# A two-layer lookup convolution: from image-by-image stages with running maxima to layer-by-layer blocks with packed 32-column products

## The chip, the cores and the metric

The kernel runs on one core of a Trainium2 chip. A core has five engines that work side by side, each with its own queue in order: TensorE (PE, matrix products into PSUM; its weight loads are listed as PEld), VectorE (DVE), ScalarE (ACT), GpSimd (POOL) and SyncE (SP, which here issues transfers). [...] The metric is the device time of one execution in microseconds (us); the median of three runs before the change is 5095.48 us (5089.49 to 5102.17).

## The reference

The input x has 16 images of 256 channels, 28 x 28 pixels. It is normalized in 32 groups of channels, and a block with two approximated 3x3 convolutions follows. Each convolution has, for every channel, 16 code vectors of 9 numbers, compares each 3x3 patch of that channel with them, and takes a soft choice:

```python
def amm_conv3x3(x, centroids, w_sub, stride=1):
    B = x.shape[0]
    C, k, s = centroids.shape                      # 256, 16, 9
    patches = conv_general_dilated_patches(x, (3, 3), (stride, stride), 'SAME')
    p = patches.reshape(B, C, s, Ho * Wo).transpose(0, 3, 1, 2)
    d = sum(p * p, -1)[..., None] - 2.0 * einsum('bncs,cks->bnck', p, centroids) + sum(centroids ** 2, -1)
    attn = softmax(-d, axis=-1)
    lut = einsum('cks,cso->cko', centroids, w_sub)
    out = einsum('bnck,cko->bno', attn, lut)
    return out.transpose(0, 2, 1).reshape(B, -1, Ho, Wo)

out = relu(bn(amm_conv3x3(gn(x), centroids1, wsub1)))
out = bn(amm_conv3x3(out, centroids2, wsub2))
out = se_layer(out)                                # channel gates from the channel means
y = x + relu(out + gn(x))
```

In both kernels the lookup is taken apart: the exponentials of a channel's 16 logits are multiplied by its code vectors (the numerators, 9 rows for a channel), these are divided by the sum of the exponentials, and the quotient is multiplied by `w_sub`. The logit of code c for patch p is 2(p.c - |c|^2/2); the term |p|^2 falls out of the softmax. All data are fp32, in which a matmul is two instructions.

## The kernel before

Channels are laid three to a strip of 32 rows (27 rows of numerators, three of sums), four strips to a stack of 128: 88 strips, 22 stacks, taken two at a time (`g`, 11 of them). An image and layer is a stage, cut into 384 and 400 pixels; layer 1 of the next image and layer 2 of this one alternate. A pair of stacks and a cut of pixels is a slot, 704 in all; a unit is two slots.

Patches come from DRAM. `shift` on POOL makes the two sideways shifts of an image, `to_home` writes three shifted images, `to_pat` (L278) copies these within DRAM into a tensor of patches with a row of ones, and `patches` (L342) loads a unit.

For a safe exponential, each channel's maximum is subtracted. This makes logits twice: `a_logits` (L355) makes them, `a_turn` (L371) turns them in blocks of 32x32 on DVE, `a_max` (L379) takes the maxima over 16 codes, and `m_turn`, `m_out` (L397) and `m_in` (L406) carry the maxima by way of DRAM (dm) into rows of the patch tile, where the second product `b_logits` (L355 again) subtracts them. `b_exp` (L420) makes the exponentials on ACT, `b_num` (L429) the numerators and, in every eighth row, the sums; `b_keep` (L442) copies them to SBUF as q. The sums go by DRAM (ds, dr; L447 to L468) into a dense tile, where `r_make` (L457, L458) inverts them, and come back; `c_scale` spreads them over the rows with a shuffle on DVE (L481) and multiplies on POOL (L482). `c_look` (L491) multiplies by `w_sub` over all stacks into two banks, and `evacuate` (L507, L517) applies the batch norm. `se_hidden`, `se_gate`, `finish` and `store` end an image.

The order on each engine is written out by hand: `at(slot, half, f)` lists every step under a slot and a position in it, and the steps are issued in sorted order. A step of slot s stands at s (first logits), s + 3 (second), s + 4 (numerators), s + 8 and s + 9 (scaling, lookup). Six PSUM banks form one ring, `bank`; two more are the lookup's accumulators.

Of the kernel before, what the change touches and what calls it, by code (L numbers as in the profile page):

```python
# [8 lines left out]
F32 = mybir.dt.float32  # L9
AF = mybir.ActivationFunctionType  # L10
# [8 lines left out]
NPAD = (H + 2) * W  # L19
K = 16  # L20
NCH = 3
NRT = 88
NT = NRT // 4
NG = NT // 2
CPAD = NRT * NCH
GN_EPS = 1e-5
BN_EPS = 1e-5

PROW = [(v, 8) for v in range(7)] + [(24, 1), (27, 1)]
ONE = 30
MROW = (7, 15, 23)

NROW = [r for r in range(32) if r % 8 != 7][:27]

PXT = ((0, 384, 0, 384), (384, 400, 368, 416))
UNITS = ((0, 2), (2, 2), (4, 2), (6, 2), (8, 2), (10, 1))  # L40


def prow(j, s):
    base, step = PROW[j * 3 + s % 3]
    return base + step * (s // 3)
# [3 lines left out]
def kernel(  # L49
# [4 lines left out]
    cw1: bass.AP,  # L54
    ws1: bass.AP,
    wd2: bass.AP,
    cw2: bass.AP,
    ws2: bass.AP,
    nhalf: bass.AP,
    mones: bass.AP,  # L60
# [6 lines left out]

# [7 lines left out]
    drot = ctx.enter_context(tc.tile_pool(name="drot", bufs=3, space=DRAM))  # L82
    small = ctx.enter_context(tc.tile_pool(name="small", bufs=3))
    p_acc = ctx.enter_context(tc.tile_pool(name="p_acc", bufs=1, space=PSUM))
    p_ring = ctx.enter_context(tc.tile_pool(name="p_ring", bufs=6, space=PSUM))
# [8 lines left out]
    def view(t, off, dims):  # L94

        return bass.AP(t.tensor, t.offset + off, [list(d) for d in dims])


    DX = CPAD * NPAD
    d_home = [dram.tile([3 * CPAD, NPAD], F32, name=f"home{i}") for i in range(2)]  # L100
    d_pat = [dram.tile([NRT * 32, HW], F32, name=f"pat{i}") for i in range(3)]
    d_zero = dram.tile([2, NPAD], F32, name="zero")
# [3 lines left out]
    xpool = ctx.enter_context(tc.tile_pool(name="xpool", bufs=2))  # L106

    def load_x(b):
        t = xpool.tile([P, NB, HW], F32, tag="xt", name="xt")
        nc.gpsimd.dma_start(t, x[b].rearrange("(b p) n -> p b n", p=P))  # L110
        xs[b] = t

    xs = {}
    load_x(0)

    def zeros(dims):
        return view(d_zero, 0, dims)

    def clear_home(i):
        t = d_home[i]
        nc.scalar.dma_start(view(t, 0, [[NPAD, 3 * CPAD], [29 * W, 2], [1, W]]), zeros([[0, 3 * CPAD], [0, 2], [1, W]]))
        nc.scalar.dma_start(view(t, C * NPAD, [[DX, 3], [NPAD, CPAD - C], [1, NPAD]]), zeros([[0, 3], [0, CPAD - C], [1, NPAD]]))

    def clear_pat(i):
        t = d_pat[i]
        nc.scalar.dma_start(view(t, 7 * HW, [[32 * HW, NRT], [8 * HW, 4], [1, HW]]), zeros([[0, NRT], [0, 4], [1, HW]]))
        nc.scalar.dma_start(view(t, ONE * HW, [[32 * HW, NRT], [1, HW]]), view(d_zero, NPAD, [[0, NRT], [1, HW]]))

    with tc.tile_pool(name="zo", bufs=1) as zpool:
        zo = zpool.tile([2, NPAD], F32, name="zo")
        nc.vector.memset(zo, 1.0)
        nc.vector.memset(zo[0:1], 0.0)
        nc.scalar.dma_start(d_zero, zo)
    clear_home(0)
    clear_pat(0)


    nc.vector.tensor_scalar_mul(gmat, gmat, 1.0 / 8.0)  # L140
    mhalf = const.tile([P, NB], F32, name="mhalf")
    nc.vector.memset(mhalf, -0.5)

    def load(ap, name):
        t = const.tile(list(ap.shape), F32, name=name)
        nc.sync.dma_start(t, ap)
        return t

    vecs = load(vec, "vecs")
    nhalf_sb = load(nhalf, "nhalf_sb")  # L150
    mones_sb = load(mones, "mones_sb")
    wd = [load(wd1, "wd0")]
    cw = [load(cw1, "cw0")]
    ws = [load(ws1, "ws0")]
    wd.append(load(wd2, "wd1"))
    cw.append(load(cw2, "cw1"))
    ws.append(load(ws2, "ws1"))
# [5 lines left out]
    nb2_sb = const.tile([P, NB], F32, name="nb2_sb")  # L163
    nc.vector.tensor_scalar_mul(nb2_sb, vecs[:, :, 8], -1.0)

    def rsqrt(dst, src, eps, n):

        t = small.tile([P, n], F32, name="rs_t")
        nc.gpsimd.tensor_scalar(t, src, eps, None, op0=ALU.add)
        nc.gpsimd.tensor_tensor(dst, t, mhalf[:, :n], ALU.pow)  # L170


    bn = []
    for l in range(2):
        ga, be, mu, va = (vecs[:, :, 4 * l + i] for i in range(4))
        sc = const.tile([P, NB], F32, name=f"bnsc{l}")
        sh = const.tile([P, NB], F32, name=f"bnsh{l}")
        rsqrt(sc, va, BN_EPS, NB)
        nc.vector.tensor_mul(sc, sc, ga)
        nc.vector.tensor_mul(sh, mu, sc)  # L180
        nc.vector.tensor_sub(sh, be, sh)
        bn.append((sc, sh))


    def setup_codes(l):
        wf = wd[l].rearrange("p t m -> p (t m)")
        n = NT * 64
        for c0 in range(0, n, 416):
            m = min(416, n - c0)
            sq = tpool.tile([P, 416], F32, tag="z", name="sq")  # L190
            nc.gpsimd.tensor_tensor(sq[:, :m], wf[:, c0 : c0 + m], wf[:, c0 : c0 + m], ALU.mult)  # L191
            ps = bank("sqp")
            nc.tensor.matmul(ps[:, :m], lhsT=nhalf_sb, rhs=sq[:, :m], start=True, stop=True)  # L193
            nc.vector.tensor_add(wf[:, c0 : c0 + m], wf[:, c0 : c0 + m], ps[:, :m])
        nc.vector.tensor_add(wd[l], wd[l], mones_sb.unsqueeze(1).to_broadcast([P, NT, 64]))

    hpool = ctx.enter_context(tc.tile_pool(name="hpool", bufs=1))
    ppool = ctx.enter_context(tc.tile_pool(name="ppool", bufs=5))
    tpool = ctx.enter_context(tc.tile_pool(name="tpool", bufs=4))
    epool = ctx.enter_context(tc.tile_pool(name="epool", bufs=6))  # L200
    npool = ctx.enter_context(tc.tile_pool(name="npool", bufs=4))
    rpool = ctx.enter_context(tc.tile_pool(name="rpool", bufs=2))
    mxs = [const.tile([P, 8, 32], F32, name=f"mx{i}") for i in range(2)]
    for t in mxs:
        nc.vector.memset(t, 0.0)

    sides = {dx: const.tile([P, NB, HW], F32, name=f"side{dx}") for dx in (0, 2)}
    for t in sides.values():
        nc.gpsimd.memset(t, 0.0)


    gst = {}
    nrm = {}

    def gn_stats(b):
        st = small.tile([P, NB, 2, 6], F32, name="gn_st")
        mv = small.tile([P, NB, 2], F32, name="gn_mv")
        for k in range(NB):
            for i in range(2):
                nc.vector.bn_stats(st[:, k, i, :], xs[b][:, k, i * (HW // 2) : (i + 1) * (HW // 2)])  # L220
            nc.vector.bn_aggr(mv[:, k, :], st[:, k])
        gst[b] = mv

    def gn_mean(b):
        mv = gst[b]
        ps = bank("gnp")[:, : 2 * NB]
        nc.tensor.matmul(ps, lhsT=gmat, rhs=mv.rearrange("p b t -> p (b t)"), start=True, stop=True)
        gm = small.tile([P, NB, 2], F32, name="gn_gm", bufs=6)
# [6 lines left out]
    def gn_var(b):  # L235
        gm, dv = gst.pop(b)
        ps = bank("gnp")[:, :NB]
        nc.tensor.matmul(ps, lhsT=gmat, rhs=dv, start=True, stop=True)
        var = small.tile([P, NB], F32, name="gn_var")
        nc.vector.tensor_add(var, gm[:, :, 1], ps)  # L240
        rstd = small.tile([P, NB], F32, name="gn_rstd", bufs=6)
        rsqrt(rstd, var, GN_EPS, NB)
        nrm[b] = gm, rstd

    homes = {}

    def gn_apply(b):
        gm, rstd = nrm[b]
        xt = xs.pop(b)
        for k in range(NB):  # L250
            nc.gpsimd.tensor_scalar(  # L251
                xt[:, k], xt[:, k], gm[:, k, 0:1], rstd[:, k : k + 1], op0=ALU.subtract, op1=ALU.mult
            )
        homes[0, b] = xt


    def pat_of(l, b):
        if l == 0:
            return d_pat[2 if b == 1 else 0]
        return d_pat[0 if b == B - 1 else 1]  # L260

    def shift(l, b, dx, k):

        img = homes[l, b][:, k].rearrange("p (r w) -> p r w", w=W)
        to = sides[dx][:, k].rearrange("p (r w) -> p r w", w=W)
        if dx == 0:
            nc.gpsimd.tensor_copy(to[:, :, 1:W], img[:, :, 0 : W - 1])
        else:
            nc.gpsimd.tensor_copy(to[:, :, 0 : W - 1], img[:, :, 1:W])

    def to_home(l, b, dx):
        src = homes[l, b] if dx == 1 else sides[dx]
        nc.gpsimd.dma_start(view(d_home[l], dx * DX + W, [[NPAD, P], [P * NPAD, NB], [1, HW]]), src)

    def to_pat(l, b, n):
        dx, j = (1, 0, 2)[n // 3], n % 3
        base, step = PROW[j * 3 + dx]
        nc.gpsimd.dma_start(  # L278
            view(pat_of(l, b), base * HW, [[32 * HW, NRT], [step * HW, 3], [1, HW]]),
            view(d_home[l], dx * DX + j * NPAD, [[3 * NPAD, NRT], [W, 3], [1, HW]]),  # L280
        )


    ys = {}
    se = {}
# [391 lines left out]
```

## Time and profile before

| what | value |
|---|---|
| median time | 5095.48 us |
| span of the profiled execution | 5090.5 us |
| busy: PE / DVE / POOL / ACT | 86 / 74 / 44 / 42 % |
| mean granted TensorE clock | 0.919 |
| instructions: all / PE | 107493 / 39696 |
| DMA packets, bytes | 698762, 885.87 MB |
| lookups L491, busy and mean of one | 2408.2 us, 552 ns |
| logits L355, busy and mean of one | 1536.6 us, 553 ns |
| products L482 on POOL, busy and mean of one | 1400.7 us, 1012 ns |
| transposes L371 on DVE | 1435.6 us, 567 ns |
| maxima L379 on DVE | 1396.0 us, 560 ns |
| exponentials L420 on ACT | 1185.8 us, 515 ns |
| first logits start at | 114.2 us |

Busy time is the union of the intervals in which an engine has some instruction under way. Matmuls overlap, so the mean length of one is longer than the distance between the starts of two in succession, and packed matmuls of different strips run at the same time. What ends an idle stretch is shown per group and in the list of waits; the chain shows through which work the last instruction was reached.

### The profile page before, as it was taken

The numbers are of one execution on the slowest core, as the hardware profiler recorded it, in microseconds if no ns is written. First come the engines' busy times: TensorE is split into PE (matmuls) and PEld (weight loads), VectorE is DVE, ScalarE is ACT, GpSimd is POOL, SyncE is SP. The second block draws the span as 40 slices with busy tenths as digits, with TensorE's granted clock in tenths as the row PEclk, the third lists the DMA queues.
The fourth block names the chain that finished last, engine by engine and source line by source line (L and its number), as shares of the span: only waits on it lengthen the run. The fifth ranks groups of instructions, "written<-read, shape, count | busy, mean of one in ns | idle before, by whom it ended". The sixth has DMA issues, their size and how long they took to land. (4 is left out here: it accounts for less than half of the span.)

```text
span 5090.5 us, 107493 instructions
## 1 busy us (share of the span) xinstructions
PE 4396.4 (86%) x39696; PEld 1579.5 (31%) x39696; DVE 3769.4 (74%) x9144; ACT 2113.9 (42%) x5265; POOL 2254.7 (44%) x2438
## 2 busy tenths in 40 slices
PE   1788898888988889898898988889888898888988
PEld 0233333333333333233333333333233333333333
DVE  1777787677877778777787876778777787777876
ACT  0344444344444444443444443444443444434444
POOL 2444445354443545434444353544444444344433
PEclk8899999899999999998899998999989999999999
DMA  6555656556465565655556565564655656565543
GB/s 227 164 174 165 193 151 194 170 175 193 143 201 166 184 191 161 189 155 180 187 159 189 156 188 181 173 194 146 199 164 174 203 149 189 166 182 184 175 136 92
DMA packets 698762, 885.87 MB, mean 174 GB/s; under 512 B 460306, under 2 KB 565922, under 8 KB 697980
## 3 DMA queue, kind: packets, MB, share of 16 engines
q0 software_dynamic: 149248, 642.59, 38.1%
q1 hardware_dynamic: 544352, 231.75, 18.2%
q8 instruction: 313, 5.13, 0.4%
q10 hardware_dynamic: 4636, 4.66, 0.4%
q14 instruction: 213, 1.74, 0.1%
HBM read 671.90 MB, written 449.80 MB: 220 GB/s over the span
## 5 line engine op out<-in xcount | busy, mean ns | idle before, releaser
L482 POOL TENSOR_TENSOR q<-q,rb 128x384 f32<-128x384 f32 (+1 forms) x1408 | 1400.7, 1012 | 2683.7 <-DVE rb L481 1091.3
L491 PE MATMUL acc<-q,ws 128*128 128x384 f32 (+1 forms) x5632 | 2408.2, 552 | 132.6 <-POOL q L482 130.9
L371 DVE STREAM_TRANSPOSE z<-lg 128x416 f32<-128x416 f32 (+1 forms) x2816 | 1435.6, 567 | 760.8 <-PE lg L355 759.0
L355 PE MATMUL lg<-pt,wd 31*64 31x384 f32 (+2 forms) x22528 | 1536.6, 553 | 462.8 <-DMA pt<-dm 296.4
L491 PEld LDWEIGHTS acc<-q,ws 128*128 128x128 f32 x5632 | 1015.2, 201 | 1533.7 <-issue 856.3
L420 ACT ACTIVATE e<-lg 128x400 f32<-128x400 f32 (+1 forms) x2816 | 1185.8, 515 | 556.5 <-PE lg L355 555.0
L379 DVE TENSOR_REDUCE mx<-z 128x26 f32<-128x416 f32 (+1 forms) x2816 | 1396.0, 560 | 0.0
L442 ACT COPY q<-nm 128x384 f32<-128x384 f32 (+1 forms) x1408 | 613.8, 488 | 1649.6 <-issue 860.6
L355 PEld LDWEIGHTS lg<-pt,wd 31*64 31x64 f32 x22528 | 400.8, 137 | 1419.1 <-DVE z L371 424.1
L481 DVE STREAM_SHUFFLE rb<-rt 128x384 f32<-128x384 f32 (+1 forms) x1408 | 772.3, 596 | 0.9
L429 PE MATMUL nm<-e,cw 64*32 64x384 f32 (+1 forms) x11264 | 652.0, 516 | 13.1 <-ACT se_hid L299 13.1
L457 ACT ACTIVATE sp<-sp 128x192 f32<-128x192 f32 (+3 forms) x384 | 141.4, 368 | 553.4 <-DMA sp<-ds 552.0
L342 POOL DMA_DIRECT2D pt<-pat x384 | 301.0, 784 | 36.3 <-DMA pat<-home 32.6
L481 DVE LOAD_MASK_SELECT rb<-rt x1408 | 19.4, 14 | 351.2 <-DMA rt<-dr 349.7
L429 PEld LDWEIGHTS nm<-e,cw 64*32 64x32 f32 x11264 | 130.4, 106 | 434.2 <-issue 371.5
L278 POOL DMA_DIRECT2D pat<-home x288 | 244.7, 850 | 38.5 <-DMA pat<-zero 29.9
L388 DVE STREAM_TRANSPOSE mt<-mx 128x256 f32<-128x256 f32 (+1 forms) x384 | 162.4, 423 | 13.2
L458 ACT ACTIVATE sp<-sp 128x192 f32<-128x192 f32 (+3 forms) x384 | 135.4, 353 | 12.2
L251 POOL TENSOR_SCALAR xt<-xt,gn_gm,gn_rstd 128x784 f32<-128x784 f32 x32 | 96.5, 3019 | 0.1
L517 ACT ACTIVATE y<-acc,bnsh,bnsc 128x384 f32<-128x384 f32 (+1 forms) x64 | 44.2, 690 | 103.7 <-PE acc L491 103.7
L507 ACT ACTIVATE h<-acc,bnsh,bnsc 128x384 f32<-128x384 f32 (+1 forms) x64 | 44.1, 690 | 71.1 <-PE acc L491 71.1
L193 PE MATMUL sqp<-sq,nhalf_sb 128*128 128x416 f32 (+1 forms) x16 | 9.2, 743 | 62.8 <-POOL sq L191 62.8
(60 smaller groups left out, 496.8 us busy)
## 6 DMA issues: line engine op xcount, KB each, us to landing
pat<-home POOLq DMA_DIRECT2D x288, 808.5 KB, 6.4
pt<-pat POOLq DMA_DIRECT2D x160, 832.0 KB, 7.9
pt<-pat POOLq DMA_DIRECT2D x160, 768.0 KB, 5.3
home<-side POOLq DMA_DIRECT2D x64, 784.0 KB, 4.4
dm<-mt SPq DMA_DIRECT2D x640, 64.0 KB, 3.7
xt<-in_x POOLq DMA_DIRECT2D x32, 784.0 KB, 7.2
pt<-dm SPq DMA_DIRECT2D x320, 50.0 KB, 2.2
ds<-q SPq DMA_DIRECT2D x160, 100.0 KB, 2.4
```

The source lines that it names most:

```text
L278: nc.gpsimd.dma_start(view(pat_of(l, b), base * HW, [[32 * HW, NRT], [step * HW, 3], [1, HW]]), view(d_home[l], dx * DX + j * NPAD, [[3 * ...
L342: nc.gpsimd.dma_start(pt[:, : 2 * ng, :wn], view(pat_of(u["l"], u["b"]), 2 * g0 * P * HW + wpx, [[HW, P], [P * HW, 2 * ng], [1, wn]]),)
L355: nc.tensor.matmul(bs[i][64 * h : 64 * h + 64, :n], lhsT=wd[l][32 * i : 32 * i + rows, 2 * g + h, :], rhs=u["pt"][32 * i : 32 * i + rows, ...
L371: nc.vector.transpose(z[:, :n], u["lg", gi][i][:, :n])
L379: nc.vector.tensor_reduce(u["mx"][:, 4 * gi + i].rearrange("p (c b) -> p b c", c=2)[:, : n // 32], z[:, :n].rearrange("p (b c k) -> p b c ...
L388: nc.vector.transpose(mt[:, : 4 * ng].rearrange("p a b -> p (a b)"), u["mx"][:, : 4 * ng].rearrange("p a b -> p (a b)"))
L420: nc.scalar.activation(e[:, :n], bk[:, :n], AF.Exp, scale=2.0)
L429: nc.tensor.matmul(bs[h][32 * i : 32 * i + 32, :n], lhsT=cw[l][64 * h : 64 * h + 64, g, i, :], rhs=e[64 * h : 64 * h + 64, :n], start=True ...
L442: nc.scalar.copy(u["q"][:, (2 * gi + h) * n : (2 * gi + h + 1) * n], bk[:, :n])
L481: nc.vector.stream_shuffle(rb[:, :n], u["rt"][:, a : a + n], MASK)
L482: nc.gpsimd.tensor_tensor(u["q"][:, a : a + n], u["q"][:, a : a + n], rb[:, :n], ALU.mult)
L491: nc.tensor.matmul(accs[key][:, :n], lhsT=ws[l][:, 2 * g + h, o * P : (o + 1) * P], rhs=u["q"][:, a : a + n], start=(g == 0 and h == 0), s ...
```

## The change

The whole schedule is rewritten. Layer 1 is done for all 16 images, then layer 2. A block is a layer, an image, half of the rows (14 x 28 = 392 pixels) and half of the channels (128): 128 blocks, of two clusters each.

- **Patches from padded images.** Each normalized image is written once to DRAM with a border of zeros, 30 x 30 a channel. Nine transfers of the SP queue load a block's patches, one for each of the nine offsets: offset s goes to rows s, s + 16, ... A channel has 16 rows, nine of them filled and one used as a constant.
- **Logits once.** A channel pair (32 rows, 32 codes) is a 32x32 tile of TensorE, so 16 of them stand in the array. The codes are centred over the 16 codes, with a constant shift, and the exponential is taken without a maximum.
- **Maxima for 32 channels only.** After image 0 of layer 1 the channels are ranked by (largest activation) x (spread of the codes), and layer 2's channels are permuted by that rank. The first 32, quarter `mm` 0 of the half `hh` 0 (a "wide" block), keep the way by transposes: copy from PSUM, transpose, maximum, subtract, transpose back, exponential over 4 x 392.
- **Guard.** Every exponential also gives its sum (`accum_out`), which POOL adds up (`watch`). If a sum or a code is too large, a loop after the blocks does everything again with maxima.
- **Sums inside the products.** Eight of the nine numerator rows of a channel come from `num_a` (64 x 32 tiles). `num_b`, four quarters accumulated into two banks, holds the ninth row and the sums of all channels; `split_b` and `join_b` bring them into a tile r of sums and a ninth tile q. One reciprocal for a block; `scale_q` spreads it with a shuffle and multiplies, both on DVE. No sum goes to DRAM.
- **18 stacks.** Eight q tiles of 128 rows and the ninth for each half: 18 lookups for an output half and row half, in place of 22. The ring has seven banks, the accumulator one.

The diff is cut to the steps of a block and their order. Set-up, ranking, the permuted weights, the repair loop and the layout of the constants are left out.

```diff
-    p_ring = ctx.enter_context(tc.tile_pool(name="p_ring", bufs=6, space=PSUM))
+    p_ring = ctx.enter_context(tc.tile_pool(name="p_ring", bufs=7, space=PSUM))
...
+    epool = ctx.enter_context(tc.tile_pool(name="epool", bufs=17))
+    qpool = ctx.enter_context(tc.tile_pool(name="qpool", bufs=31))
...
+    def patches(u, eng=None):
+        hm = (home1 if u["l"] == 0 else home2)[u["b"]]
+        for s in range(S):
+            dy, dx = divmod(s, 3)
+            (eng or nc.sync).dma_start(
+                u["pt"][s::16, :, : PTW - 2],
+                view(hm, 16 * u["hh"] * NPAD + (RT * u["t"] + dy) * PW + dx,
+                     [[32 * NPAD, 8], [NPAD, 16], [1, PTW - 2]]),
+            )
+    def logits(u, mm):
+        bs = []
+        for i in range(4):
+            bk = bank("lg")
+            for c in range(4):
+                nc.tensor.matmul(
+                    bk[32 * c : 32 * c + 32, :N].rearrange("p (r w) -> p r w", w=W),
+                    lhsT=wts["wd", u["hh"]][32 * i : 32 * i + 32, mm, c, :],
+                    rhs=u["pt"][32 * i : 32 * i + 32, 4 * mm + c, :].rearrange("p (r w) -> p r w", w=PW)[:, :, :W],
+                    start=True, stop=True,
+                )
...
+            nc.scalar.activation(e, bk[:, :N], AF.Exp, scale=2.0, accum_out=wt[:, i : i + 1])
...
+    def watch(u, mm):
+        wm = wmax[u["l"]][:, 4 * (mm % 2) : 4 * (mm % 2) + 4]
+        nc.gpsimd.tensor_tensor(wm, wm, u.pop(("wt", mm)), ALU.add)
...
+    def wide_exp(u, mm):
+        raw = u.pop(("raw", mm))
+        nc.scalar.activation(raw, raw, AF.Exp, scale=2.0)
...
+                nc.tensor.matmul(
+                    bs[r][32 * i : 32 * i + 32, :N],
+                    lhsT=wts["cwa", u["hh"]][64 * r : 64 * r + 64, mm, i, :],
+                    rhs=es[i][64 * r : 64 * r + 64, :],
+                    start=True, stop=True,
+                )
...
+    def copy_a(u, mm):
+        for r, bk in enumerate(u.pop(("na", mm))):
+            q = qpool.tile([P, N], F32, tag="q", name="q")
+            nc.scalar.copy(q, bk[:, :N])
...
+    def num_b(u):
+        bs = [bank("nb") for _ in range(2)]
+        for mm in range(4):
...
+    def split_b(u):
+        nc.scalar.activation(y, b0[:, :N], AF.Identity, bias=zero, scale=m_hi)
+        nc.scalar.activation(xx, b0[:, :N], AF.Identity, bias=zero, scale=m_lo)
...
+    def join_b(u):
+        nc.vector.scalar_tensor_tensor(r, b1[:, :N], m_lo, y, op0=ALU.mult, op1=ALU.add)
+        nc.vector.scalar_tensor_tensor(q, b1[:, :N], m_hi, xx, op0=ALU.mult, op1=ALU.add)
...
+    def recip_dve(u):
+        nc.vector.reciprocal(u["r"], u["r"])
...
+    def scale_q(u, k):
+        rb = rpool.tile([P, N], F32, tag="rb", name="rb")
+        nc.vector.stream_shuffle(rb, u["r"], mask_of(k))
+        nc.vector.tensor_mul(u["q", k], u["q", k], rb)
...
+    for j, u in enumerate(blocks):
+        wide = u["l"] == 1 and u["hh"] == 0
+        g = 2 * j
+        at(g - 3, 2.5, patches, u)
+        for p in range(2):
+            for q in range(2):
+                mm = 2 * p + q
+                at(g + p, 1.0 + 0.1 * q, logits, u, mm)
+                if wide and mm == 0:
+                    at(g, 1.02, wide_copy, u, mm)
+                    at(g, 1.03, wide_turn, u, mm)
+                    at(g, 1.04, wide_sub, u, mm)
+                    at(g, 1.05, wide_back, u, mm)
+                    at(g + 1, 0.5, wide_exp, u, mm)
+                else:
+                    at(g + p, 1.02 + 0.1 * q, exps, u, mm)
+                    at(g + p, 1.5, watch, u, mm)
+        early, late = ((1, 3), (0, 2)) if wide else ((0, 1), (2, 3))
+        if wide:
+            early, late = (1,), (2, 3, 0)
+        for mm in early:
+            at(g + 1, 0.3, num_a, u, mm)
+            at(g + 1, 0.4, copy_a, u, mm)
+        at(g + 2, 0.1, num_b, u)
+        at(g + 2, 0.15, split_b, u)
+        at(g + 2, 0.2, join_b, u)
+        for mm in late:
+            at(g + 2, 0.3, num_a, u, mm)
+            at(g + 2, 0.4, copy_a, u, mm)
+        at(g + 2, 0.25, recip_dve, u)
+        order = [2 * mm + r for mm in early + late for r in range(2)] + [8]
+        for n, k in enumerate(order):
+            at(g + 2 + (n >= 4), 1.6 if n < 4 else 0.6, scale_q, u, k)
...
+            g = 8 * (l * B + b)
+            k = g + 5
+            for t in range(2):
+                for o in range(2):
+                    for hh in range(2):
+                        u = byk[l, b, t, hh]
+                        for s in range(NS):
+                            at(k, 2.0, lookup, u, s, o, hh == 0 and s == 0, hh == 1 and s == NS - 1)
+                        k += 1
+                    at(k, 0.0, evacuate, l, b, t, o)
```

`at(cluster, position, f)` lists the steps as before; the even cluster of block j is 2j. In a cluster, TensorE's order is `num_b` of the block before (even clusters), `num_a`, two `logits`, nine `lookup`.

## The prediction

> **What bounds the kernel now.** I read the page from the top: the busy shares, the chain that ended last, the groups, then the timeline of TensorE in a stretch without disturbance.
>
> ```profile
> PE 4396.4 (86%) x39696; PEld 1579.5 (31%) x39696; DVE 3769.4 (74%) x9144; ACT 2113.9 (42%) x5265; POOL 2254.7 (44%) x2438
> PE 25%; DMA 11%; DVE 2%; issue 1%; ACT 1%; SPq 0%; POOL 0%; POOLq 0%; ACTq 0%; DVEq 0%
> core 0: 5090.5 us, clock 0.919
> ```
>
> PE is busy 86%, but the chain also passes through DMA for 11%, and the clock is not full. The timeline says what a busy PE does:
>
> ```profile
> 2523.61 0.88 PE L429 MATMUL nm<-e,cw 64*32 64x384 f32 x16
> 2524.42 0.90 PE L355 MATMUL lg<-pt,wd 31*64 31x384 f32 x16
> 2525.25 1.56 PE L491 MATMUL acc<-q,ws 128*128 128x384 f32 x4
> 2526.74 0.95 PE L355 MATMUL lg<-pt,wd 31*64 31x416 f32 x16
> 2527.62 1.56 PE L491 MATMUL acc<-q,ws 128*128 128x384 f32 x4
> 2529.11 0.55 PE L429 MATMUL nm<-e,cw 64*32 64x384 f32 x8
> ```
>
> Columns: start, length, group, instructions. An fp32 matmul is two instructions, or passes. From start to start, numerators take 0.81 us, logits 0.83 to 0.88, a pair of lookups 1.49. A slot (logits twice, numerators once, two lookup pairs) is 2 x 0.83 + 0.81 + 2 x 1.49 = 5.45 us; 704 slots make 3837 us. Two narrower windows give the pass: successive lookups start at 2525.68 and 2526.00, so 384 columns take 0.32 us, 4 passes 1.29 us, and the other 0.20 us of the 1.49 is the change of shape. Eight packed matmuls cost 2 passes (0.64) + 0.17: the packing is complete, also where four streams share the same rows (numerators).
>
> The other 1250 us are waits, and the half clock that follows them. The list of waits names them:
>
> ```profile
> POOL q L482 <- DVE rb L481: 1091.3, 286, 11.1
> ACT sp L457 <- DMA sp<-ds: 552.0, 192, 10.2
> PEld lg L355 <- DVE z L371: 424.1, 653, 4.0
> DVE rb L481 <- DMA rt<-dr: 349.7, 102, 8.3
> PEld lg L355 <- ACT e L420: 313.6, 568, 1.1
> PE lg L355 <- DMA pt<-dm: 296.4, 129, 8.8
> PEld acc L491 <- POOL q L482: 279.8, 235, 6.0
> ```
>
> So each unit of two slots goes twice out to DRAM and back (maxima by dm, sums by ds and dr), and PE meets those round trips. The kernel is bound by PE work plus a chain of latencies between four engines and the DMA queue.
>
> [...]
>
> **The change on PE.** There are 128 blocks (2 layers, 16 images, 2 row halves, 2 channel halves), N = 392 columns, so a pass is 0.32 x 392/384 = 0.329 us. Per block: `logits` 4 x 16 tiles of 32x32, 8 passes; `num_a` 4 x 8, 8 passes; `num_b` 4 x 8, 8 passes; `lookup` 18, 36 passes. Sixty passes make 19.7 us. A block has two clusters, each with three changes of shape: 6 x 0.19 = 1.1. Sum **20.9 us** without waits; over 128 blocks 2675 us against 3837. The second logits for all channels (704 x 0.83 = 584 us) and 22 to 18 stacks in the lookup are what went.
>
> **ACT per block.** Spacing, not length, counts: four L420 in 1.69 us with a length of 0.52 gives (1.69 - 0.52)/3 = 0.39. The accumulated sum is new on `exps`: L517 shows a further read of 193 ns; with the overlap I take 0.51 each (bounds 0.39 and 0.72). 16 x 0.51 = 8.2; eight copies at 0.38 = 3.0; `split_b`, with scale and bias tensors as in L517 (0.68 long), 2 x 0.57 = 1.1; evacuation 0.6. Sum **12.9**, below PE.
>
> **DVE per block.** The shuffle takes 0.50 (two L481 in succession); a product of SBUF operands, by the reduction's and STT's slope, 0.48; nine of each = 8.8. `join_b` 2 x 0.5 = 1.0. The reciprocal of 392: [...] I take 3.3. Sum **13.1**; normalization adds 0.7. In layer 2 every other block has the wide path: two transposes, a reduction and a subtraction over 1568, 4 x 1.68 = 6.7, so 19.8, still below PE. All maxima's transposes and reductions (1435.6 + 1396.0 us) leave DVE, and the products (L482) leave POOL for DVE.
>
> **What waits remain.** Sums now lie in PSUM rows and are spread by shuffles: no DRAM round trip. Scaled q are needed two clusters later, so DVE lags hidden. What I see ending last is the ring of seven PSUM banks. An even cluster takes 14 banks. By hand, from the start of `num_b`: it ends at 2.7; `split_b` on ACT runs 2.8 to 3.9, behind which the copies are queued; `num_a` ends at 4.1; copies 3.9 to 5.5; the first exp 5.5 to 6.0. The eighth logits bank of the cluster is the first one of the same cluster, so PE starts it at 6.1 (release to start 0.11 us, as after L420), instead of at about 5; logits end at 6.8, then nine lookups of 0.66 and a change: **12.8**. `join_b` at 3.9 to 5.2 holds the third bank, which is earlier. Odd cluster: numerators to 14.2; the evacuation stands ahead of the copies on ACT (12.9 to 13.5), copies 13.7 to 15.3, first exp 15.9, last bank 16.0 to 16.7, lookups to **22.7**. So a block takes 22.7, of which 1.8 is waiting.
>
> Layer 2, a pair of blocks: the wide exp of 1568 (1.5 us) stands ahead of the exps and itself waits for DVE (join 5.1, reciprocal 8.4, wide path to 15.1), which moves the last bank from 16.0 to 17.1; in the next block two more copies move it by 0.75. 2 x 22.7 + 1.9 = **47.3**. Per image, `finish` puts two 1.0 us ACT passes before the copies: 1.8 us. `watch` on POOL is tiny, but four buffers let ACT run only two clusters ahead of it; POOL's scatters are once only.
>
> **Patches.** Nine SP transfers per block, each 128 runs of 1672 B; [...] at the 67 to 86 ns of 1600 B runs in this trace, 10 to 12 us. They are issued when the block two before has read the buffer, 33 us ahead of need. Hidden. The homes written as padded images end the shifts, the three copies and L278's transfers, all off the path.
>
> **The sum.** Layer 1: 64 x 22.7 = 1453. Layer 2: 32 x 47.3 = 1514. `finish` 16 x 1.8 = 29; means and ranking/permutation set-up, 35. Start 48 (x in 7, statistics 3, loads ahead of the first home on the same queue, home 5, patches 12; before, the first logits came at 114.2). End 30. Wake-ups of waiting instructions, two in a cluster at 0.1: 50. Sum 3159; I say **3150 us**.
>
> **Rivals.**
> 1. Sixteen tiles don't overlap: four streams in each of four row strips at once is new; eight is what the trace shows. If logits take double, +4 x 0.66 = 2.64 us per block, 338 in all: **3490**.
> 2. Patches bind: if the nine transfers of eight partitions land one after another at the 3.7 us of pt<-dm, a block takes 33.3 us: 4262 + 100 = **4360**. Against it: transfers of one queue overlap in this trace, and run times are short.
> 3. Slower: the in-order queues couple so that PE, ACT and DVE take turns. 20.9 + 12.9 + about 17 = 50.8 us a block, **6500 us**; the same side if the repair loop after the blocks were taken. For it: PE today loses 1250 us to such waits. Against: every consumer stands one or two clusters behind its producer, and even PE and ACT strictly in turn give 33.8, below today's 5090/128 = 39.8.
>
> **How the numbers follow.** Forecast 0.68; rival 1 0.14; rival 2 0.12; rival 3 0.06. The range 2880 to 3700: the lower end is PE nearly without waits (2675 + ends and set-up 200), the upper holds rival 1 with 200 us to spare for waits that I sized too small. Beyond it lie rivals 2 and 3 and a little. Faster by over 0.3%: 0.93; within: 0.01; slower: 0.06.
>
> **What would show it.** Right: sixteen logits matmuls (32 passes) in some 0.7 us; lookups 0.33 us apart; no DMA worth naming on the chain; PE waits by ACT's exps and copies, about 1 us per cluster; clock near 1; the reciprocal near 3.3 us without effect; ACT near 60% and DVE near 70% busy. Wrong: logits groups of 1.3 us; PE waiting for patches; PE gaps ended by DVE's wide path or `join_b` over 2 us; a half clock kept by many short stalls.

## The result, and the profile after

The changed kernel takes **3271.14 us** (median of 4 runs, 3264.05 to 3282.79) where the kernel before takes 5098.82 on the same chip: ratio 0.641, 95% interval 0.6387 to 0.6432. The forecast was 3150 in a range of 2880 to 3700. So the direction and the mechanism held; some 120 us were missed, most of them at the seams (start, set-up, ends of images), as the table below shows.

The page's busy shares, clock and chain come first.

```profile
span 3281.3 us, 89800 instructions
PE 3104.1 (95%) x37648; PEld 1475.6 (45%) x37648; DVE 2122.6 (65%) x4356; ACT 1717.3 (52%) x5553; POOL 300.1 (9%) x664
PEclk9889899999999999999999999999999999999998
PE 85%; DMA 6%; ACT 4%; DVE 2%; issue 2%; POOL 1%; SPq 0%; ACTq 0%; POOLq 0%; DVEq 0%
```

PE has gone from 25% of the chain to 85%; DMA is left with 6%, most of it start and set-up. POOL fell from 2254.7 us to 300.1, DVE from 3769.4 to 2122.6. One block of layer 1, in PE's timeline (start, length, group, instructions):

```profile
1015.27 2.86 PE L362 MATMUL nb<-e,cwb 64*32 64x392 f32 x64
1017.93 1.52 PE L342 MATMUL na<-e,cwa 64*32 64x392 f32 x32
1019.38 3.06 PE L286 MATMUL lg<-pt,wd 32*32 32x392 f32 x64
1022.37 6.19 PE L407 MATMUL acc<-q,ws 128*128 128x392 f32 x18
1028.49 1.55 PE L342 MATMUL na<-e,cwa 64*32 64x392 f32 x32
1029.97 2.58 PE L286 MATMUL lg<-pt,wd 32*32 32x392 f32 x64
1032.48 6.19 PE L407 MATMUL acc<-q,ws 128*128 128x392 f32 x18
1038.60 2.86 PE L362 MATMUL nb<-e,cwb 64*32 64x392 f32 x64
```

From start to start: `num_b` 2.66, `num_a` 1.45, logits 2.99, nine lookups 6.12, then 1.48, 2.51, 6.12. The block is 23.33 us, 13.22 and 10.11 for its clusters. A cluster's logits are two groups of sixteen tiles, four passes: 4 x 0.329 and a change of shape of 0.2 are 1.52, so 1.47 us of the first and 0.99 of the second are waiting, though PE counts as busy (that sixteen tiles need no longer is shown by look_between below). What PE's weight loads (PEld, 37,648 for as many matmuls) wait for stands in the list of waits (total, times, longest) and on the timelines of PEld and ACT in the even cluster:

```profile
PEld lg L286 <- ACT e L300: 137.7, 218, 3.3
PEld lg L286 <- ACT q L353: 121.0, 425, 0.8
```

```profile
1021.09 0.15 PEld L286 LDWEIGHTS lg<-pt,wd 32*32 32x32 f32 x8 [0.23 <-ACT q L353]
1021.58 0.15 PEld L286 LDWEIGHTS lg<-pt,wd 32*32 32x32 f32 x8 [0.34 <-ACT e L300]
```

```profile
1018.25 0.68 ACT L373 ACTIVATE y<-nb,kst 128x392 f32<-128x392 f32 x1 [6.59 <-PE nb L362]
1018.83 0.67 ACT L375 ACTIVATE x<-nb,kst 128x392 f32<-128x392 f32 x1
1019.39 1.64 ACT L353 COPY q<-na 128x392 f32<-128x392 f32 x4
1020.89 0.55 ACT L300 ACTIVATE e<-lg 128x392 f32<-128x392 f32 x1
1021.28 0.25 ACT L300 ACTIVATION_READ_ACCUMULATOR e<-lg 128x1 f32 x1
1021.37 0.54 ACT L300 ACTIVATE e<-lg 128x392 f32<-128x392 f32 x1
```

`split_b`, then the copies, then the first exponential, which ends at 1021.44; the last strip of logits starts at 1021.58, in the bank it set free. The strip before it waited for a copy (`q`). That is the ring of seven banks, as worked out by hand. The rest of the page's sizes: lookups 0.33 apart, exponentials 0.47 apart (taken: 0.51), copies 0.38, the reciprocal

```profile
L389 DVE RECIPROCAL r<-r 128x392 f32<-128x392 f32 x128 | 331.9, 2593 | 0.0
```

2.59 us instead of 3.3.

**Where 3150 became 3271.** The profiled span is 3281.3 us. Cut at the starts of `num_b`, in us, beside the terms of the forecast (its 50 for wake-ups put to the blocks):

| part | forecast | measured | how |
|---|---|---|---|
| to the first `num_b` | 48 | 62 | first logits at 53.4, not 48; filling the pipeline 8.7 |
| 128 blocks, undisturbed | 3017 | 3028 | 64 x 23.33 + 32 x 47.96 |
| set-up and means, layer 1 | 35 | 77 | layer 1 takes 1570.5, less 64 x 23.33 |
| ends of images, layer 2 | 29 | 83 | layer 2 takes 1617.4, less 32 x 47.96 |
| end | 30 | 31 | |

The undisturbed blocks came out within 0.4%. What was missed lies at the seams.

### The profile page after: what moved, and what is told of

It is laid out like the page before. It is cut to its first block, busy times and chain, and to the rows that moved or that the text cites. A ratio compares the mean times of both kernels' runs of the same rounds, so it can differ in the third digit from the quotient of the medians.

```text
span 3281.3 us, 89800 instructions
## 1 busy us (share of the span) xinstructions
PE 3104.1 (95%) x37648; PEld 1475.6 (45%) x37648; DVE 2122.6 (65%) x4356; ACT 1717.3 (52%) x5553; POOL 300.1 (9%) x664
## 4 chain that ended last, share of the span: by engine, by line
PE 85%; DMA 6%; ACT 4%; DVE 2%; issue 2%; POOL 1%; SPq 0%; ACTq 0%; POOLq 0%; DVEq 0%
PE acc L407 46%; PE lg L286 18%; PE nb L362 10%; PE na L342 10%; DMA pt<-home 1%; DMA xt<-in_x 1%; DMA st<-in_wsub 1%; ACT e L300 1%; DMA st<-in_sk 1%; ACT raw L334 1%; ACT q L353 1%; ACT y L610 1%; DMA d_sc<-score 0%; ACT y L428 0%; DVE rb L399 0%
## 5 line engine op out<-in xcount | busy, mean ns | idle before, releaser
L407 PE MATMUL acc<-q,ws 128*128 128x392 f32 x4608 | 1625.2, 508 | 1.9 <-ACT y L428 1.7
L300 ACT ACTIVATE e<-lg 128x392 f32<-128x392 f32 x1920 | 935.1, 557 | 106.3 <-PE lg L286 96.5
L286 PE MATMUL lg<-pt,wd 32*32 32x392 f32 x16384 | 750.7, 505 | 135.9 <-ACT e L300 45.9
L400 DVE TENSOR_TENSOR q<-q,rb 128x392 f32<-128x392 f32 x1152 | 654.7, 568 | 67.4 <-ACT q L353 0.9
L399 DVE STREAM_SHUFFLE rb<-r 128x392 f32<-128x392 f32 x1152 | 681.2, 591 | 0.0
L300 ACT ACTIVATION_READ_ACCUMULATOR e<-lg 128x1 f32 x1920 | 516.8, 269 | 0.0
L353 ACT COPY q<-na 128x392 f32<-128x392 f32 x1024 | 422.5, 505 | 37.8 <-PE na L342 31.9
L342 PE MATMUL na<-e,cwa 64*32 64x392 f32 x7680 | 378.2, 496 | 0.0
L362 PE MATMUL nb<-e,cwb 64*32 64x392 f32 x7680 | 347.6, 494 | 0.0
L389 DVE RECIPROCAL r<-r 128x392 f32<-128x392 f32 x128 | 331.9, 2593 | 0.0
```

The source lines that it names most:

```text
L286: nc.tensor.matmul(bk[32 * c : 32 * c + 32, :N].rearrange("p (r w) -> p r w", w=W), lhsT=wts["wd", u["hh"]][32 * i : 32 * i + 32, mm, c, : ...
L300: nc.scalar.activation(e, bk[:, :N], AF.Exp, scale=2.0, accum_out=wt[:, i : i + 1])
L342: nc.tensor.matmul(bs[r][32 * i : 32 * i + 32, :N], lhsT=wts["cwa", u["hh"]][64 * r : 64 * r + 64, mm, i, :], rhs=es[i][64 * r : 64 * r + ...
L353: nc.scalar.copy(q, bk[:, :N])
L362: nc.tensor.matmul(bs[r][32 * i : 32 * i + 32, :N], lhsT=wts["cwb", u["hh"]][64 * r : 64 * r + 64, mm, i, :], rhs=es[i][64 * r : 64 * r + ...
L389: nc.vector.reciprocal(u["r"], u["r"])
```

## The experiments

The theory after the result was: PE's work sets the time; in each cluster the last logits wait for ACT, and the rest is lost at seams. Rivals: patches bind after all; the sixteen tiles overlap only in part; the guard's sums on ACT are what PE waits for; DVE's load is near its limit. The runs are spread over several chips, on which the kernel before took 5107 to 5129 us; each ratio is to the kernel before on the same chip.

**look_between** and **look_first** only move lookups within a cluster. In the kernel after, all nine follow the logits; here four, or five, stand ahead of them (and, in look_between, two between the two quarters), so that ACT frees banks meanwhile. Work and data stay the same. The comments in the diff name the kernel.

```diff
-                            at(k, 2.0, lookup, u, s, o, hh == 0 and s == 0, hh == 1 and s == NS - 1)
+                            w = 0.9 if s < 4 else 1.08 if s < 6 else 2.0     # look_between
+                            w = 0.9 if s < 5 else 2.0                        # look_first
+                            at(k, w, lookup, u, s, o, hh == 0 and s == 0, hh == 1 and s == NS - 1)
```

> The nine lookups of a cluster are cut into 4, 2 and 3, with the two logits groups between them. Theory (the ring of seven PSUM banks: logits wait for copies and for the cluster's own first exponential): the copies are long done when logits begin, so the 2.5 us of waits in a block of 23.33 us go, and three more changes of shape per cluster (0.19 us each, 1.1 us a block) come: 22.0 us a block, about 3100 us in all. Rival (the sixteen-tile logits are themselves slow, 2.5 to 3.0 us for two groups, whatever the banks do): only the changes are added, 24.5 us a block, about 3420 us.

> Five lookups stand before the logits, four after. Theory of the ring: one more change of shape per cluster (0.38 us a block) and only the wait of the last bank for the first exponential left (0.65 us a cluster): 22.6 us a block, about 3170 us. Rival (slow sixteen-tile logits): 23.7 us a block, about 3320 us.

look_between: 3056.91 us, ratio 0.5971 (0.5961 to 0.5981). look_first: 3173.64, 0.6196 (0.6185 to 0.6206). PE in look_between:

```profile
1040.18 0.94 PE L286 MATMUL lg<-pt,wd 32*32 32x392 f32 x32
1041.05 1.58 PE L407 MATMUL acc<-q,ws 128*128 128x392 f32 x4
1042.56 0.94 PE L286 MATMUL lg<-pt,wd 32*32 32x392 f32 x32
1043.43 2.24 PE L407 MATMUL acc<-q,ws 128*128 128x392 f32 x6
```

A quarter's sixteen tiles (32 instructions) take 0.87 us from start to start: two passes are 0.66, the change of shape 0.21. The sixteen tiles overlap completely, and rival 1 of the prediction is gone. The block is 22.11 us: 60 passes of 0.329 and twelve changes of 0.2 are 22.1, so no wait is left, although six more changes were bought. The sum shows this, and the busy share doesn't. A stretch of layer 2 in look_between and one of layer 1 in the kernel after, which has the waits, look alike (window, us, busy PE, PEld, DVE, ACT, POOL with instructions, clock, DMA share, GB/s):

```profile
1700.00:2900.00 1200.00, 1198.93 (x15580) 517.00 (x15584) 957.66 (x1778) 755.95 (x2315) 46.56 (x186) 1.00 0.51 104
1000.00:1600.00 600.00, 599.89 (x7447) 289.52 (x7446) 363.24 (x830) 327.77 (x1104) 78.63 (x153) 1.00 0.51 111
```

Layer 2's pairs fell from 47.96 to 45.3 and 45.6. Between the first and the last `num_b` 227 us went: 158 in the blocks (64 x 1.22 and 32 x 2.5), and nearly all the rest at the ends of images in layer 2, which cost about 5 us in the kernel after and 0.5 here. So the ends, too, were a wait of the ring. look_first takes the two apart. Its two quarters of logits still stand together, take 2.42 us in either cluster for 1.52 and so wait for banks, and the block is 23.07; the ends of images, though, cost 0.5 us as well. Lookups ahead of the logits cure the ends, lookups between the quarters the blocks.

**no_watch** leaves out the guard's sums (the exponentials have no accumulator output, nothing adds up); the outputs are otherwise made as before.

```diff
-            nc.scalar.activation(e, bk[:, :N], AF.Exp, scale=2.0, accum_out=wt[:, i : i + 1])
+            nc.scalar.activation(e, bk[:, :N], AF.Exp, scale=2.0)
...
-                    at(g + p, 1.5, watch, u, mm)
```

> Leaves out the guard: exponentials give no sums, so the 1920 reads of the accumulator (516.8 us busy on ScalarE) and the adding-up on GpSimd go. Theory of the ring: only the first exponential of each cluster stands in front of the last bank, and its release comes at most 0.1 us earlier: 3245 to 3270 us. Rival (ScalarE's load of 52% is what sets the block): 0.09 us for each of 16 exponentials of a block, 1.4 us a block, 3100 us or less.

3259.31 us, 0.637 (0.6349 to 0.639), 0.6% below the kernel after, the intervals just touching. The sums are nearly free. Exponentials stand 0.38 us apart instead of 0.47, but PE waits only for the first of a cluster: each cluster's logits take 0.08 to 0.09 us less (2.90 and 2.43 for 2.99 and 2.51), and the block 23.16 for 23.33. That fits the ring and not a bound by ACT's load, which would have given 1.4 us a block.

**patch2q** lets GpSimd's queue carry four of the nine offsets.

```diff
-            (eng or nc.sync).dma_start(
+            (eng or (nc.gpsimd if 4 <= s < 8 else nc.sync)).dma_start(
```

> Four of the nine patch transfers of a block (offsets 4 to 7) go out from GpSimd's queue instead of SyncE's. Theory (patches hidden: 20.5 us from first issue to landing, needed after 33): a block stays at 23.33 us; only the ranking's round trip, which stood behind patches on one queue, may become shorter: 3240 to 3275 us. Rival ([...]): blocks under 22.5 us, 3150 us or less.

3314.9 us, 0.6471 (0.646 to 0.6482): 1% slower than the kernel after, and so a miss. Undisturbed blocks are still 23.33 us, with the SyncE part landing in 14 us, from its first packet to its last, where all nine transfers took 19.2. So the length of a patch load doesn't bind. The loss lies in 18 gaps of PE, up to 5.9 us and 52.7 us in all, for which the trace names no releaser (the kernel after has 6, of 13.3 us); the last section comes back to them.

**wide_off** leaves out the maxima of the 32 ranked channels in layer 2 (with a small scale in their exponential, so that nothing overflows): the wide path as a whole.

```diff
+            sc = 0.01 if u["l"] == 1 and u["hh"] == 0 and mm == 0 else 2.0
...
-        wide = u["l"] == 1 and u["hh"] == 0
+        wide = False
```

> Leaves out the maxima of the 32 ranked channels in layer 2: their logits go through the plain exponential, scaled by 0.01 in place of 2, so that they stay finite. Theory: a pair of blocks in layer 2 falls from 47.96 us to twice 23.33: 32 x 1.3 = 42 us, about 3230 us. Rival (the wide path's 7 us on VectorE delay more than the pair shows, for instance at the end of an image): 3180 us or less.

3222.95 us, 0.6274 (0.6248 to 0.6301). Layer 2's blocks become 23.33 each, so the maxima cost 1.3 us a pair, 41 us in all; the forecast had 1.9. The profiled layer 2 is 60 us shorter. The other 19 lie almost all at the ends of images, as the rival had it in part.

**fin_pool** moves the affine pass at the end of an image from ACT to GpSimd.

```diff
-        nc.scalar.activation(y, y, AF.Identity, bias=nrm[:, b, 2, k : k + 1], scale=gt[:, k : k + 1])
+        nc.gpsimd.tensor_scalar(y, y, gt[:, k : k + 1], nrm[:, b, 2, k : k + 1], op0=ALU.mult, op1=ALU.add)
```

> The affine pass of the end of an image (two of 1.04 us per image, ahead of the copies on ScalarE) goes to GpSimd, about 3 us each by its row for 128x784. Theory: layer 2's extra of some 5 us per image is these two passes in front of the first exponential, 2 us, and the half clock that PE falls into after the longer wait: 16 x 3 to 5 us less, 3190 to 3225 us. Rival (the extra comes from VectorE's four products per image or from the gate): 3260 to 3280 us, no change.

3236.68 us, 0.63 (0.6274 to 0.6325), 1.7% below the kernel after, somewhat less than expected. An image's end cost about 5 us and now costs 2.5. In the kernel after it looks like this on ACT and then on PE:

```profile
2300.20 1.04 ACT L610 ACTIVATE y<-y,nrm,se_gt 128x784 f32<-128x784 f32 x1
2301.13 1.65 ACT L353 COPY q<-na 128x392 f32<-128x392 f32 x4
2302.63 1.09 ACT L610 ACTIVATE y<-y,nrm,se_gt 128x784 f32<-128x784 f32 x1
2303.58 0.53 ACT L300 ACTIVATE e<-lg 128x392 f32<-128x392 f32 x1
```

```profile
2304.25 0.90 PE L286 MATMUL lg<-pt,wd 32*32 32x392 f32 x8 [0.55 <-ACT e L300]
2305.08 7.80 PE L407 MATMUL acc<-q,ws 128*128 128x392 f32 x18
```

Both passes stand ahead of the first exponential, PE runs dry, and the nine lookups after it take 7.73 us from start to start instead of 6.12: the first five are 0.65 us apart instead of 0.33, at half the clock. So the wait can be paid a second time in clock, but it isn't always. Three images earlier the same place looks the same and the lookups take 6.12:

```profile
2001.78 0.86 PE L286 MATMUL lg<-pt,wd 32*32 32x392 f32 x8 [0.56 <-ACT e L300]
2002.57 6.19 PE L407 MATMUL acc<-q,ws 128*128 128x392 f32 x18
```

The block with an image's end takes 26.6, 28.2 or 29.8 us in 13 of 15 images, with 0, 3.4 or 6.8 us at half clock within it; an undisturbed one in that place takes 24.1. So an end costs 2.5 us at full clock and 0 to 3.4 more by the clock (the last section says what decides). Two such blocks, of 26.6 and 29.9 us (columns as above, the clock third from the end):

```profile
1982.10:2008.70 26.60, 25.91 (x318) 11.90 (x314) 18.37 (x38) 15.96 (x51) 1.07 (x4) 1.00 0.32 70
2182.60:2212.50 29.90, 29.21 (x316) 13.28 (x312) 18.36 (x37) 15.96 (x51) 1.09 (x4) 0.89 0.34 81
```

**rank_q** sends the ranking's two small transfers by GpSimd's queue, out from behind the patches in SyncE's.

```diff
-        nc.sync.dma_start(view(d_sc, o * P, [[1, P], [1, 1]]), score[:, o : o + 1])
+        nc.gpsimd.dma_start(view(d_sc, o * P, [[1, P], [1, 1]]), score[:, o : o + 1])
...
-        nc.sync.dma_start(row[:, :C], view(d_sc, 0, [[0, P], [1, C]]))
+        nc.gpsimd.dma_start(row[:, :C], view(d_sc, 0, [[0, P], [1, C]]))
```

> The scores' way to DRAM and back goes out from GpSimd's queue in place of SyncE's. Theory: the one gap of 23 us near 230 us is the row of scores [...]; then some 15 to 20 us are won, about 3252 us. Rival (the ranking's own chain on VectorE and the look-up of the permutation make the gap): no change.

3280.98 us, 0.6386 (0.636 to 0.6413): no change. The 128 scores of 4 bytes, issued near 206 us, landed some 16 us later again. The queue isn't what delays them; what does wasn't isolated.

**recip2** adds two reciprocals to each block, 5.2 us of DVE time, with results that nobody reads.

```diff
+        for i in range(2):
+            spare = rpool.tile([P, N], F32, tag="rb", name="spare")
+            nc.vector.reciprocal(spare, u["r"])
```

> Two more reciprocals per block into a spare tile, 5.2 us of VectorE a block, ahead of the scaling. Theory (consumers stand a cluster or two behind): layer 1 unchanged at 23.33 us a block, layer 2 up by 0 to 1.5 us a pair where the wide exponential waits for VectorE: 3270 to 3320 us. Rival (VectorE, 65% busy, is close to the bound): up to 5.2 x 128 = 665 us more.

3654.47 us, 0.7116 (0.7088 to 0.7144): my expectation fell. DVE has 644 us more of busy time (2767.0 for 2122.6), and the kernel takes 383 us more (374 between the profiled spans), with DVE at 76% and so still idle in part. Layer 1's blocks stay at 23.33 us except one an image (31.05), where PE's small matmul of the group means, in order ahead of the work behind it, waits 5.15 us for DVE's statistics. In layer 2 the blocks during which a wide path runs go from 24 us to 31, seven for 5.2 added: the wide exponential waits for DVE, and the exponentials behind it on ACT hold PE's banks. The block at an image's end, 26.6 to 29.9 us in most images before, takes some 31. About half of the seven is clock again: such a block has 6.8 us or more at half clock, which is up to 3.4 us lost.

The first two lines are of recip2 as a whole; in the kernel after, the first of these waits doesn't occur, and the second is 45.9 us in 49 waits. The other two are of the kernel after, where the wide path ended 0.23 us before ACT came to its exponential: that was the whole reserve.

```profile
ACT raw L334 <- DVE raw L330: 142.0, 30, 5.0
PE lg L286 <- ACT e L300: 182.9, 36, 6.2
```

```profile
2069.49 1.81 DVE L330 STREAM_TRANSPOSE raw<-z 128x1568 f32<-128x1568 f32 x1
2071.53 1.52 ACT L334 ACTIVATE raw<-raw 128x1568 f32<-128x1568 f32 x1
```

The idle third of DVE hid nothing where PE, ACT and DVE stand in a row, each in order, and everything in the other blocks of layer 1.

**all_max** takes the maxima back for all channels in layer 2, one quarter after the other within its cluster, with four exponentials of 392 in place of the one of 1568; it leaves out the guard's sums there. Layer 1 is unchanged.

```diff
-        wide = u["l"] == 1 and u["hh"] == 0
+        wide = u["l"] == 1
...
-                if wide and mm == 0:
+                if wide:
```

> Undoes one part for layer 2: every channel of both halves takes the wide path (copy, transpose, maximum, subtraction, transpose back, exponential), without the guard's sums; layer 1 as in the change. Theory (not taking maxima is what keeps VectorE off the path): four wide paths of 7.2 us and 13.5 us of other work make 42 us of VectorE in a block, and one raw buffer chains copy, path and exponential to about 44 us: 3271 + 64 x 19 = 4490 us. Rival (the gain lies in the sums without DRAM and in fewer matmuls, and VectorE would hide this): under 3700 us.

5264.87 us, 1.0292 (1.0265 to 1.0319) of the kernel before. It missed by far: a block of layer 2 takes 56 us and not 42 to 44. ACT's timeline shows much of it:

```profile
3000.11 1.79 ACT L337 ACTIVATE e<-raw 128x392 f32<-128x392 f32 x4 [10.74 <-DVE raw L330]
3001.93 1.65 ACT L312 COPY raw<-lg 128x392 f32<-128x392 f32 x4
3011.01 1.79 ACT L337 ACTIVATE e<-raw 128x392 f32<-128x392 f32 x4 [7.43 <-DVE raw L330]
```

One buffer `raw` is copied to, turned, turned back, exponentiated, 10.9 us from one exponential to the next, and one quarter after the other: that is the chain of the forecast. From cluster to cluster the step is 16 or 17 us instead of 10.9, which the forecast left out: there the numerators on PE and their copies on ACT stand between one quarter's exponentials and the next copy to `raw`. More buffers weren't tried. In this order of work the maxima in layer 2 alone use up the whole gain. The page of all_max has DVE at 71% and PE at 70% (77 and 60% within layer 2): neither is a bound by its load.

**best1, best2, best3** join what helped. All have look_between's positions and fin_pool's edit, and the group means later on PE. best1 also puts layer 2's reciprocal behind the wide path and the ranking later; best2 further sends x and layer 2's weights by GpSimd's queue. The diff is cut: the steps that follow the ranking move with it, and x and the codes have the same edit as `wsub2`.

```diff
-                    at(g + 2, 2.1, gn_mean, b + 1)
+                    at(g + 3, 0.95, gn_mean, b + 1)                                        # all three
-        at(g + 2, 0.25, recip_dve, u)
+        at(g + 2, 1.3 if u["l"] == 1 and u["hh"] == 1 else 0.25, recip_dve, u)             # best1, best2
-                        at(g + 13, 0.03, rank_make, o)
+                        at(g + 14, 1.7, rank_make, o)                                      # best1, best2
-        nc.sync.dma_start(st[:, :n], wsub2[o * P : (o + 1) * P, part * 4 * C : part * 4 * C + n])
+        nc.gpsimd.dma_start(st[:, :n], wsub2[o * P : (o + 1) * P, part * 4 * C : part * 4 * C + n])  # best2
```

> Lookups around the logits (as in look_between), the end's affine pass on GpSimd, the means' first matmul a cluster later, the ranking a cluster later, and in layer 2 the reciprocal after the wide path. Theory (what look_between leaves are waits of single steps: 1.35 us per image for the means, 23 us once for the ranking, some 2.5 us per image in layer 2): 15 + 15 + 25 us less than 3057, about 3000 us. Rival (these waits only move to the next step in the same queue): 3045 us or more.

> best1, and the loads of x in layer 1 and of the second layer's weights go out from GpSimd's queue. Theory ([...] VectorE or GpSimd wait for them): 10 to 25 us less than best1, all of it before 520 us. Rival (as with the ranking's transfer, [...]): no change.

> look_between with the means' first matmul a cluster later and the end's affine pass on GpSimd; the reciprocal and the ranking stay where the change has them. Theory (best1 lost in layer 2, where the later reciprocal holds back the join and with it the third PSUM bank; its other moves were sound): 17 us from the means and 5 to 10 us from the ends of images, 3030 to 3040 us. Rival (the affine pass on GpSimd is what cost best1 its gain): 3050 us or more.

best1 3067.34 us, 0.5997 (0.5984 to 0.6011); best2 3064.5, 0.5991 (0.5977 to 0.6005); best3 3050.34, 0.597 (0.596 to 0.598). best1 and best3 missed their forecasts (3000, and 3030 to 3040), and best2 is no faster than best1, as its rival had it. With the later means the block that holds them takes 22.34 us where look_between has 23.46, once an image in 11 images, as expected. But in best1 layer 2 gets slower than in look_between, 23.88 and 24.12 us where that has 23.09 and 23.62: the reciprocal had run while DVE waited for the copies anyway, and put later it delays the scaling and the next `join_b`, so that PE's weight loads wait for the latter (9.7 us, 19 times between 1900 and 2800 us, absent there in look_between). best3 takes this move back and is at look_between's times again. And the ranking moved its wait instead of losing it: PE now waits 21.2 us for the evacuation. best3, without these two moves, has the lowest time, but is no faster than look_between by the intervals: of the 12 us that the means give, its first block takes back 7 (41.11 us where look_between has 34.08), and fin_pool adds nothing, since an image's end costs 0.5 us in both.

## Why the prediction was right, and where it was off

- **PE work, 20.9 us a block: right.** Pass 0.329, change of shape 0.2, sixteen tiles in two passes, all as taken. look_between's 22.11 is that sum with six more changes, so PE is the bound when the wait is taken away. That sixteen tiles overlap no run had shown before; their two passes took 0.66 us beside the change of shape of 0.21.
- **Where the 1828 us went.** By the prediction's sums, PE's own work fell from 3837 to 2675 us, and the runs bear out the second figure; the other 670 are fewer waits and less half clock. Which part of the change (sums kept on chip, logits once, no maxima, both products on DVE) took away which wait wasn't tested one by one. all_max alone undoes one of them, and its single buffer adds a wait of its own.
- **The ring of seven banks as the last wait: right**, even cluster 12.8 by hand and 13.22 measured, odd 9.9 and 10.11, the release of the first exponential where it was put. The wake-ups counted apart (0.4 us a block) make 23.1 for 23.33.
- **Layer 2's pair, 47.3 and 0.8 of wake-ups: right** at 47.96. The number is right and the step partly: the wide exponential stands ahead of others on ACT, as argued, but it didn't wait for DVE, which was done 0.23 us before in 28 of 32 cases. So the cost is 1.3 us by wide_off and not 1.9; recip2 brought the wait about.
- **End of an image, 1.8 us: mis-sized, 5.** I counted the two ACT passes and not the lowered clock that can follow the wait. At full clock an end costs 2.5 us; on top of that come 72 us at half clock between layer 2's first and last `num_b`, which make some 36 us lost, an estimate from the trace of the kernel after. fin_pool gets half of the end's cost back, look_between nearly all: 7 us at half clock are left there.
- **Set-up and means, 35 us: mis-sized, 77.** The ranking alone holds PE for 23 us (DVE waits 20.4 us for a row of scores that goes to DRAM and back beside patches), and three blocks between 354 and 494 us take 24 us more than others, while layer 2's weights are made (PE's gaps there are ended by patches, ACT, DVE and, one of 3.1 us, by nothing that the trace shows). Two blocks near 600 us lose 5, the first two 11, the last one, at the change of layer, 8, and the means 0.47 an image.
- **Start, 48 us: 53 to the first logits**, and 8.7 us of filling, which had no term.
- **Reciprocal, 3.3 us: 2.59**, off. The 3.3 was my estimate, which no run had shown: the kernel before has the instruction on two elements only (L315, 166 ns). 2.59 us is 6.6 ns an element. That it is without effect holds in layer 1 by recip2, where three of four blocks don't change with 5.2 us more; in layer 2 the wide path stands behind it, with 0.23 us to spare.
- **Patches, 10 to 12 us and hidden: hidden is right, the size is wrong.** From the first issue to the last landing 20.5 us in the median, 141 ns a run of 1672 B instead of 67 to 86. How many of a block's 1152 runs go at once was my assumption; in the kernel after it is mostly eight or nine (79% of the time in which any is under way). They are issued 33 us ahead, which leaves room for the error; with the size so wrong, "hidden" was in part luck. 1152 runs, eight at once, at the mean of 136 ns are 19.6 us, an estimate, of look_between's block of 22.11: PE's work has little further to fall before the patches bind. Why a run takes so long isn't settled: patch2q had 140 ns too.
- **Rivals.** 1 fell by look_between's 0.87 us, 2 by patch2q's blocks of 23.33 and look_between's of 22.11. 3 did not happen, but recip2 and all_max show its beginning: with two more reciprocals, or the maxima, ACT waits for DVE and PE for ACT.
- **What I didn't see at all**: that the order of lookups and logits within a cluster decides whether the ring's wait is paid. The wait was in my working, with lookups of other data, ready to fill it, behind it in the same queue; 7% lay there, with the ends of images.

## What to carry to other kernels

Where an in-order engine waits for a buffer that another engine frees, look for work in its own queue that needs nothing new, and put it ahead of the wait: two lines were worth 7%, six more changes of shape included. Price a chain of in-order engines by its latency, not by the load of each: with DVE 65% busy, 5.2 us more on it cost 7 us in some blocks, about half of it by the clock, and none in others. And in a forecast give seams (start, set-up, ends of stages) a timeline of their own, with a range for the lower clock that may follow a wait; the steady state was right to 0.4%, the seams were short by 110 us.

## What the runs showed of the hardware

- **A wait can cost twice, and needn't.** At the ends of 15 images in the kernel after PE waits alike, with a gap of 0.55 or 0.56 us behind logits that started singly as banks came free, which count as busy. Five of these gaps have no half clock around them, four 3.4 us and six 6.8. Their place in time tells which: every change of the clock in this trace (46 stretches) lies on one grid of 3.41333 us, to 0.002 us, and so do those of the kernel before (270). Gaps that end 0.41 to 0.93 us after a point of the grid have none, those that end 2.71 to 2.84 after one have 3.4 us, and those at 3.06 to 3.12 or 0.27 to 0.28 have 6.8, without an exception; between 0.93 and 2.71 none fell. So here the second cost of a wait was chance in a single case and could only be forecast as a mean. In all, 174 us of the kernel after ran at half clock (mean clock 0.973), 820 of the kernel before (0.919) and 562 of recip2 (0.923).
- **Some gaps of PE follow packets of the instruction queue.** In the kernel after PE has 6 gaps without a releaser, 13.3 us in all. Five of them (0.5 to 3.5 us, 10.3 in all) each end 1.5 to 1.8 us after a packet of 16,384 bytes has landed in the instruction queue; the sixth (3.1 us) has none in the 8 us before its end. The queue carried 299 such packets, so most of them are followed by no such gap. This is a coincidence in time, not an experiment. In patch2q PE has 18 gaps without a releaser, 52.7 us, and the 39 us more than in the kernel after are about what it lost; why there are more with patches on GpSimd's queue stays open.
- **A small transfer was no faster on another queue.** In the one place tried, 128 scores of 4 bytes took about 16 us beside the patches, by SyncE's queue and by GpSimd's.
- **An accumulator output costs an exponential 0.09 us** (0.47 instead of 0.38 apart), though the read that goes with it is listed with 269 ns: most of it overlaps the next exponential. no_watch, without the output, has 0.38.
